# Latent attention: first tiles on free bytes, GpSimd's order written out, a batch's norm moved ahead; first attention: one mask for four diagonal tiles

## The chip, the cores and the metric

The kernel runs on one core of a Trainium2 chip. The metric is the device time of one launch in microseconds (us). Engines are named as in the profile: PE (TensorE matmuls), PEld (its weight loads), DVE (VectorE), ACT (ScalarE), POOL (GpSimd), SP (SyncE, which issues the DMAs). Every engine works through its own queue in order and waits on semaphores for the others.

## The reference

Eight residual layers over x of shape (4, 1024, 128), each applied to a layer norm of x: an attention with a learned position kernel, a mixture of experts (MoE), a linear attention, the same MoE, the latent attention, an expert layer, an attention with relative positions, the same expert layer. The change touches the first and the fifth.

```python
# first attention: 16 heads, causal
scores = jnp.take(causal_kern, jnp.maximum(doff, 0), axis=-1)
scores = scores + qm[..., :, None] + km[..., None, :]
scores = scores + MIX * jnp.einsum('bhic,bhjc->bhij', qc, kc) / math.sqrt(CR)
scores = jnp.where(causal, scores, -1000000000.0)
attn = jax.nn.softmax(scores, axis=-1)
...
# latent attention: 16 heads, causal
c_q = x @ W_DQ
Qc = (c_q @ W_UQ).reshape(B, S, N_HEADS, D_H).transpose(0, 2, 1, 3)
Qr = rope((c_q @ W_QR).reshape(B, S, N_HEADS, D_HR).transpose(0, 2, 1, 3))
c_kv = x @ W_DKV
Kr = jnp.broadcast_to(rope((x @ W_KR)[:, None, :, :]), (B, N_HEADS, S, D_HR))
scores = jnp.clip(jnp.einsum('bhqd,bhkd->bhqk', Q, K), -80.0, 80.0)
scores = jnp.where(causal, scores, -jnp.inf)
weights = jax.nn.softmax(scores / jnp.sqrt(jnp.float32(d_qk)), axis=-1)
attn = jnp.einsum('bhqk,bhkd->bhqd', weights, V)
...
```

## The kernel before

Activations stay in SBUF: 128 tokens on the partitions, eight such tiles for a batch, four batches. In both attentions a "group" is four heads of one batch (16 groups), worked side by side on PE in four blocks of 32 rows. A group has twelve units: the queries come in two halves i of 512 tokens, the keys in tiles jt of 128; half 0 has units jt = 0 to 3, half 1 has jt = 0 to 7. Where the key tile lies in the query half's own range, the unit is cut to the queries that can see it (widths 512, 384, 256, 128) and its first 128 columns are masked causally.

**First attention** (`attn0_heads`). The softmax here takes the row maxima from the scores without the position term. So each slot of the loop holds one "top", which computes scores only to find their maxima, and, ten slots behind (`LEAD`), one `weigh`, which computes the scores again with keys on the partitions, exponentiates them on ACT and multiplies the position factor on POOL (L746); `contract`, three slots later (`LAG`), multiplies by the values on PE (L754). A top is four heads' products (L680) into two score buffers of two PSUM banks each (`pair()`, three of them in all), and one DVE reduce for each buffer (L697). `tops` lists (it, c): query tile it = 0 to 7 against its own half's keys up to and with the diagonal (c = 0, widths 128 to 512; keys lie in reversed order, so the diagonal tile comes first), and for it above 3 against the whole first half (c = 1). For c = 0, four bf16 matmuls (L689) add the causal mask `after` (0 or -1e30) to the 128 diagonal columns. The negated maxima go to `maxima[0]` for it below 4; for the others to `parts`, from which a small reduce (L699) takes the minimum into `maxima[1]`. Five slots into a group `shift(0)`, and at its end `shift(1)`, transposes the maxima on PE (L705) and adds them to the queries (L706).

**Latent attention** (`attn2`). A batch is prepared in pieces: `stats` twice (DVE, L1427 and L1428), `scale` (a square root on ACT, L1436, with its table load; a reciprocal on DVE, L1439; eight multiplications into `xn` on POOL, L1442), and for each half `turn` (transposes, L1458), `latents` (L1475; two copies by ACT into `lq` and `lk`, then two DVE products and one POOL add for the rotary keys, L1467 to L1470), `rotate` (L1483, the same for the rotary queries) and `values` (L1490). Each group projects its heads in four pieces (L1545, L1546). A unit is `weigh` (L1556), a clamp on DVE (two instructions, L1567), an exp on ACT (L1570), for units 0 to 3 and 8 to 11 a causal select on POOL (L1573), and `contract` three units later (L1588). `at(n, piece)` hangs a piece on unit n; a batch's eleven pieces hang on units -22 to -12 before its first. At the end of a batch twelve more pieces divide, turn back and project its output. The pieces take their PSUM from a pool of two banks, of which the running sums of a group hold one.

PE, DVE and ACT follow the order in which the program is written inside `tc.manual_schedule`; POOL is left to the scheduler, and so are, on DVE and ACT, instructions of neighbouring layers, which may be put in between. Tiles get fixed bytes from pools stacked from the left (attentions) or the right (MoE and expert layers); a tile whose bytes were another layer's waits for that layer's last use of them. `vals`, `lq` and `lk` are cleared by POOL at the start (L1389 to L1391), two buffers each. Neighbouring layers share the small tiles of the layer norm (`ln_st`, `ln_mv`, `ln_rs`, two buffers each).

Of the kernel before, what the change touches and what calls it, by code (L numbers as in the profile page):

```python
# [36 lines left out]
P = 128  # L37
# [210 lines left out]
def hybrid_kernel(ctx: ExitStack, tc: tile.TileContext, x, out, blocks, dram, upto=8):  # L248
# [295 lines left out]
    def attn0_heads(W, xn, table, rest):  # L544
# [7 lines left out]
        LEAD, LAG = 10, 3  # L552
        tops = [(it, c) for it in range(TB) for c in range(1 + it // 4)]
        units = [(i, jt) for i in range(2) for jt in range(4 * i + 4)]
        N = len(units)
        with layer_pool("a0h", 2) as pool, layer_pool("a0k", 1) as keep:

            maxima = [keep.tile([P, 4, P], F32, name=f"maxima{n}") for n in range(2)]
            vals = [keep.tile([P, TB, H * 16 + 16], F32, name=f"vals{n}") for n in range(2)]
            for n in range(2):  # L560
                nc.gpsimd.memset(maxima[n], 0.0)
                nc.gpsimd.memset(vals[n], 1.0)
# [83 lines left out]
            class Group:  # L646
# [24 lines left out]

                def top(self, it, c):


                    i = it // 4
                    w = (it % 4 + 1) * P if c == 0 else 512
                    both = [pair().rearrange("p (k w) -> p k w", k=2) for _ in range(2)]
                    for h in range(4):
                        r = slice(32 * h, 32 * h + 32)
                        mm(  # L680
                            both[h // 2][:, h % 2, 0:w],
                            self.q[i][r, (it % 4) * P : (it % 4 + 1) * P],
                            self.k[i - c][r, 512 - w : 512],
                            start=True,
                            stop=c > 0,
                        )
                    if c == 0:
                        for h in range(4):
                            mm(both[h // 2][:, h % 2, 0:P], ident16, after, start=False, stop=True)  # L689
                    if it == 4 and c == 0:  # L690
                        self.parts = pool.tile([P, 4, 4, 2], F32, name="parts")
                    for hp in range(2):
                        if i == 0:
                            o = maxima[0][:, it, 64 * hp + 10 : 64 * hp + 64 : 32]
                        else:
                            o = self.parts[:, it - 4, 2 * hp : 2 * hp + 2, c]
                        nc.vector.tensor_reduce(o, both[hp][:, :, 0:w], AX.X, ALU.max, negate=True)  # L697
                    if it == TB - 1 and c == 1:
                        nc.vector.tensor_reduce(maxima[1][:, :, 10:P:32], self.parts, AX.X, ALU.min)  # L699

# [672 lines left out]
    def attn2(W):  # L1373
# [7 lines left out]
        N = len(units)  # L1381
        with layer_pool("a2", 2) as pool, layer_pool("a2k", 1) as keep:
            vals = [keep.tile([P, TB, H, 32], F32, name=f"vals{n}") for n in range(2)]


            lq = [keep.tile([P, S], F32, name=f"lq{n}") for n in range(2)]
            lk = [keep.tile([64, S], F32, name=f"lk{n}") for n in range(2)]
            for n in range(2):
                nc.gpsimd.memset(vals[n], 1.0)  # L1389
                nc.gpsimd.memset(lq[n], 0.0)  # L1390
                nc.gpsimd.memset(lk[n], 0.0)  # L1391
            extras = {}

            begun, spare = [], []
# [12 lines left out]
            class Batch:  # L1407
# [27 lines left out]
                def scale(self):  # L1435
                    nc.scalar.activation(self.rs, self.rs, AF.Sqrt)  # L1436

                    def later():
                        nc.vector.reciprocal(self.rs, self.rs)  # L1439
                        self.xn = pool.tile([P, TB, D], F32, name="xn", bufs=1)  # L1440
                        for t in range(TB):
                            nc.gpsimd.tensor_scalar(  # L1442
                                self.xn[:, t, :],
                                self.x[:, t, :],
                                self.mv[:, t, 0:1],
                                self.rs[:, t : t + 1],
                                ALU.subtract,
                                ALU.mult,
                            )

                    return later

                def turn(self, i):
                    if i == 0:
                        self.xT = pool.tile([P, S], F32, name="xT", bufs=1)
                    ps = free()
# [155 lines left out]
            for k, group in enumerate(groups[1:], 1):  # L1612
                for j, piece in enumerate(group.pieces):
                    at(N * k - 8 + 2 * j, piece)
                if group.g == 0:
                    for j, piece in enumerate(group.batch.pieces):
                        at(N * k - 22 + j, piece)
            for batch in batches:
                for j, piece in enumerate(batch.ends):
                    at(4 * N * (batch.b + 1) + LAG - 1 + j, piece)  # L1620
            engines = mybir.EngineType
            with tc.manual_schedule(engines={engines.PE, engines.DVE, engines.Activation}):
                first = batches[0]
                for piece in first.pieces[0:3]:
                    run([piece])
                for piece in (first.turn, first.latents, first.rotate):
                    for i in range(2):
                        run([lambda: piece(i)])
# [434 lines left out]
```

## Time and profile before

| | us |
|---|---|
| median of 3 runs | 3723.33 (3722.66 to 3723.78) |
| the profiled execution, whole | 3725.8 |
| its span, first to last instruction | 3724.1 |
| PE busy | 3537.6 (95%) |
| DVE busy | 2079.6 (56%) |
| ACT busy | 1963.5 (53%) |
| POOL busy | 919.6 (25%) |
| mean granted PE clock | 0.974 |
| first attention's heads | about 88 to 853 |
| second MoE layer | about 1402 to 1556 |
| latent attention | about 1556 to 2131 |

The profile is of one execution. A busy PE is not PE at its peak: matmuls are pipelined, their ends are modelled, and a group of them that waits in its middle is shown stretched. The chain of waits follows the work back from the last instruction, at each step to what released it, and gives start, length and what it was ("x8" is eight instructions). In the timeline a bracket holds the idle time of the engine before the instruction and what ended it. Idle time of an engine that nothing waits for costs nothing.

### The profile page before, as it was taken

How to read it: one execution, taken by the hardware profiler on the slowest of the kernel's cores; microseconds unless marked ns; L12 is line 12 of the kernel's file. 1: busy time of each engine (PE TensorE's matmuls, PEld its weight loads, DVE VectorE, ACT ScalarE, POOL GpSimd, SP SyncE). 2: the span in 40 equal slices, each digit the busy share in tenths (PEclk: the TensorE clock that was granted, in tenths of full speed). 3: DMA queues.
4: the chain of work that ended last, by engine and by line, in shares of the span. 5: the costliest groups of instructions: out<-in, count | busy, mean ns of one | idle time of the engine just before them, and what ended most of it. 6: DMA issues, size and time to landing. Idle time of an engine off the chain costs nothing.

```text
span 3724.1 us, 62175 instructions
## 1 busy us (share of the span) xinstructions
PE 3537.6 (95%) x25288; PEld 2046.6 (55%) x25288; DVE 2079.6 (56%) x4986; ACT 1963.5 (53%) x3383; POOL 919.6 (25%) x704
## 2 busy tenths in 40 slices
PE   7999999998999998899999999999999998999999
PEld 3344444436665556633333367666766766766777
DVE  5666666666553445367777721366566566566311
ACT  5455555556422214366666664466566566566543
POOL 4677777772013210222222100001001001000000
PEclk9999999999999999889999999999999999999999
DMA  3111111100520004300000000110111011010000
GB/s 100 43 46 46 46 46 46 46 24 22 142 59 1 1 15 116 91 1 1 1 1 1 14 1 1 58 35 26 33 35 35 24 35 35 24 35 24 4 9 12
DMA packets 95975, 124.31 MB, mean 33 GB/s; under 512 B 3660, under 2 KB 78028, under 8 KB 94536
## 3 DMA queue, kind: packets, MB, share of 16 engines
q1 hardware_dynamic: 95688, 120.33, 10.5%
q8 instruction: 199, 3.26, 0.4%
q14 instruction: 88, 0.72, 0.1%
HBM read 117.59 MB, written 2.73 MB: 32 GB/s over the span
## 4 chain that ended last, share of the span: by engine, by line
PE 83%; DVE 7%; ACT 5%; POOL 2%; issue 1%; DMA 1%; SPq 0%; ACTq 0%; DVEq 0%; POOLq 0%
PE mm L1929 8%; PE s L1879 8%; PE av L1716 6%; PE mm L1706 6%; PE av L1947 6%; PE s L680 5%; PE s L716 5%; PE s L1556 4%; PE av L754 3%; PE av L1097 3%; PE mm L1081 3%; PE av L1588 3%; DVE p L1567 3%; PE av L1545 2%; ACT p L1914 2%; PE av L1306 2%
## 5 line engine op out<-in xcount | busy, mean ns | idle before, releaser
L746 POOL TENSOR_TENSOR p<-p,bias 128x1536 f32<-128x1536 f32 x192 | 504.0, 2629 | 80.3 <-ACT p L728 69.6
L1897 DVE CUSTOM_DVE_ANT_0 p<-s,bias 128x512 f32<-128x512 f32 (+3 forms) x768 | 387.3, 551 | 131.4 <-PE s L1879 124.3
L1567 DVE TENSOR_SCALAR p<-s 128x1024 f32<-128x1024 f32 (+3 forms) x384 | 349.0, 952 | 94.7 <-PE s L1556 93.5
L1914 ACT ACTIVATE p<-p,tops 128x128 f32<-128x128 f32 (+7 forms) x512 | 395.6, 774 | 2.7 <-DVE tops L1897 1.9
L1929 PE MATMUL mm<-ident,p 128*128 128x128 f32 x2304 | 348.8, 284 | 36.1 <-ACT p L1914 32.2
L1934 ACT COPY pt<-mm 128x512 f32<-128x512 f32 (+1 forms) x352 | 185.9, 528 | 368.5 <-PE mm L1929 368.3
L1929 PEld LDWEIGHTS mm<-ident,p 128*128 128x128 f32 x2304 | 249.7, 141 | 173.2 <-issue 64.6
L1570 ACT ACTIVATE p<-p 128x2048 f32<-128x2048 f32 x192 | 281.0, 1483 | 88.8 <-DVE p L1567 85.9
L725 ACT ACTIVATE p<-s 128x1024 f32<-128x1024 f32 x192 | 155.8, 811 | 320.1 <-PE s L716 319.8
L1716 PEld LDWEIGHTS av<-wt,hid 128*128 128x128 f32 x2048 | 263.9, 192 | 107.1 <-issue 107.1
L1962 POOL COPY wide_rec<-rec 128x512 f32<-128x512 f32 x64 | 39.4, 616 | 1120.8 <-DVE rec L1960 1118.3
L697 DVE TENSOR_REDUCE parts<-s 128x2 f32<-128x1024 f32 (+3 forms) x256 | 251.0, 1020 | 105.7 <-PE s L680 59.9
L1879 PE MATMUL s<-keys,q 64*128 64x512 f32 (+3 forms) x1536 | 303.6, 514 | 4.0 <-DVE tops L1897 4.0
L1947 PE MATMUL av<-pt,vals 128*64 128x128 f32 x4608 | 295.2, 278 | 0.0
L1707 ACT ACTIVATE hid<-mm,wt 128x512 f32<-128x512 f32 x256 | 170.8, 691 | 220.7 <-PE mm L1706 220.1
L1947 PEld LDWEIGHTS av<-pt,vals 128*64 128x64 f32 x4608 | 248.8, 137 | 49.6 <-issue 38.5
L1716 PE MATMUL av<-wt,hid 128*128 128x128 f32 x2048 | 264.7, 275 | 0.0
L1706 PE MATMUL mm<-xT,wt 128*128 128x512 f32 x512 | 261.7, 602 | 2.5 <-ACT hid L1707 2.0
L1936 DVE COPY pt<-mm 128x512 f32<-128x512 f32 (+1 forms) x288 | 189.8, 659 | 131.6 <-PE mm L1929 131.3
L1556 PE MATMUL s<-q,k 32*128 32x512 f32 (+3 forms) x1536 | 244.8, 559 | 5.3 <-DVE p L1567 4.0
L680 PE MATMUL s<-k,q 32*128 32x512 f32 (+3 forms) x1536 | 222.8, 536 | 10.6 <-DVE parts L697 5.9
L716 PE MATMUL s<-q,k 32*128 32x512 f32 (+3 forms) x1536 | 224.2, 537 | 0.5 <-ACT p L728 0.3
(398 smaller groups left out, 5386.8 us busy)
## 6 DMA issues: line engine op xcount, KB each, us to landing
root<-roots SPq DMA_DIRECT2D x128, 256.0 KB, 6.1
bias<-rel_dram SPq DMA_DIRECT2D x32, 1024.0 KB, 5.5
bias<-pos_dram SPq DMA_DIRECT2D x16, 1536.0 KB, 7.1
bias<-pos_dram SPq DMA_DIRECT2D x16, 512.0 KB, 8.0
wt<-w_ffn SPq DMA_DIRECT2D x2, 2132.0 KB, 8.1
wt<-w_ffn SPq DMA_DIRECT2D x2, 1192.0 KB, 5.2
wt<-w_attn SPq DMA_DIRECT2D x1, 2336.0 KB
x_sb<-x SPq DMA_DIRECT2D x4, 512.0 KB, 6.9
```

Of the source, the lines that this page charges most:

```text
L680: mm(both[h // 2][:, h % 2, 0:w], self.q[i][r, (it % 4) * P : (it % 4 + 1) * P], self.k[i - c][r, 512 - w : 512], start=True, stop=c > 0,)
L716: mm(both[h // 2][:, h % 2, 0:w], self.k[jt // 4][r, (3 - jt % 4) * P : (4 - jt % 4) * P], self.q[i][r, w0:512], start=True, stop=True,)
L746: nc.gpsimd.tensor_tensor(d, d, self.bias[:, 0:3, u : u + w], ALU.mult)
L1556: mm(both[h // 2][:, h % 2, 0:w], self.k[r, jt * P : (jt + 1) * P], self.q[r, 512 * i + w0 : 512 * (i + 1)], start=True, stop=True,)
L1567: nc.vector.tensor_scalar(pt[:, 2 * hp : 2 * hp + 2, 0:w], both[hp][:, :, 0:w], 80.0, -80.0, ALU.min, ALU.max)
L1706: mm(ps, W("w1")[:, c * P : (c + 1) * P], self.batch.xT[:, self.i * 512 : (self.i + 1) * 512], start=True, stop=True)
L1716: mm(o, self.hid[:, c, t * P : (t + 1) * P], W("w2")[:, c * P : (c + 1) * P], start=(c == 0), stop=(c == C - 1))
L1879: mm(s[:, kk, 0:e], self.q[r, it * P : (it + 1) * P], keys[self.n][r, S - n + c : S - n + c + e], start=True, stop=True,)
L1897: nc.vector.tensor_tensor_reduce(out=self.p[it][:, kk, c : c + e], in0=s[:, kk, 0:e], in1=self.bias[:, kk, c : c + e], scale=-1.0, scalar= ...
L1914: nc.scalar.activation(p, p, AF.Exp, bias=self.top[it][:, kk : kk + 1], scale=-1.0, accum_out=self.sums[:, it, kk : kk + 1])
L1929: nc.tensor.transpose(ps[:, m, kk, :], self.p[it][:, kk, (m0 + m) * P : (m0 + m + 1) * P], ident)
L1947: mm(self.acc[64 * kk : 64 * kk + 64, (it % 4) * P : (it % 4 + 1) * P], vals[self.n][:, it - m0 - m, :], pt[:, m, kk, :], start=(m0 + m == 0),
```

## The change

Four edits:

1. First attention: the twelve tops of a group are listed anew. The four diagonal tiles of a half become one top (`"diagonal"`): sixteen products of 128 keys into the two score buffers, one tile for each 128 columns, then four mask matmuls of 512 columns (`after` repeated four times), then two reduces that give a maximum for each tile. The keys before the diagonal tile in the own half (`"own"`, widths 128, 256, 384) and the first half's keys for the second (`"before"`, 512) are tops with no mask. All maxima go to `parts[i]`, now kept for the whole layer and set to the largest value once, and a small reduce follows for both halves.
2. Latent attention, bytes: the long-lived tiles' pool is opened first and so lies leftmost, with `xn` and `xT` (now single, kept tiles) and `lq`, `lk` ahead of `vals`.
3. Latent attention, POOL: its engine joins the written order. Clearing `vals[0]` stands behind the first batch's norm, clearing `vals[1]` hangs on unit 4.
4. Latent attention, pieces: a batch's eleven pieces hang on units -36, -35, -34 (statistics and norm), -29 (turn), -27 (latents), -25 (rotate), -23 (values) for the first half, and -22, -19, -13, -11 for the second.

```diff
-        tops = [(it, c) for it in range(TB) for c in range(1 + it // 4)]
+        tops = [("diagonal", 0)] + [("own", it) for it in (1, 2, 3)] + [("diagonal", 1), ("before", 4)]
+        tops += [(kind, it) for it in (5, 6, 7) for kind in ("own", "before")]
...
+            parts = [keep.tile([P, 4, 4, 2 + n], F32, name=f"parts{n}") for n in range(2)]
             for n in range(2):
+                nc.gpsimd.memset(parts[n], -LOWEST)
...
+                def top(self, kind, n):
                     both = [pair().rearrange("p (k w) -> p k w", k=2) for _ in range(2)]
...
+                    if kind == "diagonal":
+                        for t in range(4):
+                            for h in range(4):
+                                r = slice(32 * h, 32 * h + 32)
+                                mm(
+                                    both[h // 2][:, h % 2, t * P : (t + 1) * P],
+                                    self.q[i][r, t * P : (t + 1) * P],
+                                    self.k[i][r, (3 - t) * P : (4 - t) * P],
+                                    start=(t == 0),
+                                    stop=False,
+                                )
                         for h in range(4):
-                            mm(both[h // 2][:, h % 2, 0:P], ident16, after, start=False, stop=True)
+                            mm(both[h // 2][:, h % 2, :], ident16, wide(after, 4), start=False, stop=True)
+                    else:
+                        w, keys = (t * P, self.k[i]) if kind == "own" else (512, self.k[0])
...
                     for hp in range(2):
+                        if kind == "diagonal":
+                            o = parts[i][:, :, 2 * hp : 2 * hp + 2, 0].rearrange("p t h -> p h t")
+                            x = both[hp].rearrange("p k (t w) -> p k t w", t=4)
                         else:
+                            o = parts[i][:, t, 2 * hp : 2 * hp + 2, 1 if kind == "own" else 2]
+                            x = both[hp][:, :, 0:w]
+                        nc.vector.tensor_reduce(o, x, AX.X, ALU.max, negate=True)
+                    if kind != "diagonal" and n == (3 if i == 0 else 7) and (i == 0 or kind == "before"):
+                        nc.vector.tensor_reduce(maxima[i][:, :, 10:P:32], parts[i], AX.X, ALU.min)
...
-        with layer_pool("a2", 2) as pool, layer_pool("a2k", 1) as keep:
-            vals = [keep.tile([P, TB, H, 32], F32, name=f"vals{n}") for n in range(2)]
+        with layer_pool("a2k", 1) as keep, layer_pool("a2", 2) as pool:
+            normed = keep.tile([P, TB, D], F32, name="xn")
+            turned = keep.tile([P, S], F32, name="xT")
             lq = [keep.tile([P, S], F32, name=f"lq{n}") for n in range(2)]
             lk = [keep.tile([64, S], F32, name=f"lk{n}") for n in range(2)]
+            vals = [keep.tile([P, TB, H, 32], F32, name=f"vals{n}") for n in range(2)]
             for n in range(2):
-                nc.gpsimd.memset(vals[n], 1.0)
                 nc.gpsimd.memset(lq[n], 0.0)
                 nc.gpsimd.memset(lk[n], 0.0)
+            def clear(n):
+                nc.gpsimd.memset(vals[n], 1.0)
...
                 if group.g == 0:
-                    for j, piece in enumerate(group.batch.pieces):
-                        at(N * k - 22 + j, piece)
+                    for j, piece in zip((36, 35, 34, 29, 27, 25, 23, 22, 19, 13, 11), group.batch.pieces):
+                        at(N * k - j, piece)
...
-            with tc.manual_schedule(engines={engines.PE, engines.DVE, engines.Activation}):
+            with tc.manual_schedule(engines={engines.PE, engines.DVE, engines.Activation, engines.Pool}):
                 first = batches[0]
                 for piece in first.pieces[0:3]:
                     run([piece])
+                clear(0)
+                at(4, lambda: clear(1))
```

More of the change, by code (lines that the diff above doesn't have):

```diff
@@ L670, in keys @@
                     nc.scalar.activation(self.k[i], ps, AF.Identity, bias=W("bk")[:, self.g : self.g + 1])
-                def top(self, it, c):
-                    i = it // 4
-                    w = (it % 4 + 1) * P if c == 0 else 512
+                def top(self, kind, n):
                     both = [pair().rearrange("p (k w) -> p k w", k=2) for _ in range(2)]
[L678 to L687, printed above, removed]
-                        for h in range(4):
-                            mm(both[h // 2][:, h % 2, 0:P], ident16, after, start=False, stop=True)
-                    if it == 4 and c == 0:
-                        self.parts = pool.tile([P, 4, 4, 2], F32, name="parts")
+                    i = n if kind == "diagonal" else n // 4
+                    t = n % 4
+                    if kind == "diagonal":
[9 more added lines that the diff above has]
+                                )
+                        for h in range(4):
+                            mm(both[h // 2][:, h % 2, :], ident16, wide(after, 4), start=False, stop=True)
+                    else:
+                        w, keys = (t * P, self.k[i]) if kind == "own" else (512, self.k[0])
+                        for h in range(4):
+                            r = slice(32 * h, 32 * h + 32)
+                            mm(
+                                both[h // 2][:, h % 2, 0:w],
+                                self.q[i][r, t * P : (t + 1) * P],
+                                keys[r, 512 - w : 512],
+                                start=True,
+                                stop=True,
+                            )
@@ L692, in top @@
                     for hp in range(2):
-                        if i == 0:
-                            o = maxima[0][:, it, 64 * hp + 10 : 64 * hp + 64 : 32]
-                        else:
[L696 to L699, printed above, removed]
+                        if kind == "diagonal":
+                            o = parts[i][:, :, 2 * hp : 2 * hp + 2, 0].rearrange("p t h -> p h t")
+                            x = both[hp].rearrange("p k (t w) -> p k t w", t=4)
+                        else:
+                            o = parts[i][:, t, 2 * hp : 2 * hp + 2, 1 if kind == "own" else 2]
+                            x = both[hp][:, :, 0:w]
@@ L1439, in later @@
                         nc.vector.reciprocal(self.rs, self.rs)
-                        self.xn = pool.tile([P, TB, D], F32, name="xn", bufs=1)
+                        self.xn = normed
                         for t in range(TB):
@@ L1453, in turn @@
                 def turn(self, i):
-                    if i == 0:
-                        self.xT = pool.tile([P, S], F32, name="xT", bufs=1)
+                    self.xT = turned
                     ps = free()
```

## The prediction

> **What bounds the kernel now.** I read the busy times first (PE 95% of the span), then the busy times by stage, since one share over eight layers says nothing about two of them.
>
> ```profile
> 88.00:853.00 765.00, 742.73 (x5655) 299.50 (x5652) 511.08 (x746) 394.25 (x706) 578.45 (x325) 0.99 0.13 44
> 1556.00:2131.00 575.00, 527.60 (x3557) 182.44 (x3556) 407.33 (x592) 364.24 (x343) 131.74 (x180) 0.93 0.01 5
> ```
>
> After the window: its length, then busy us of PE, PE's loads, DVE, ACT, POOL, then the granted clock. The first attention (first line) is PE's: 742.7 of 765 us at a clock of 0.99. The latent attention (second) has 47 us without PE and a clock of 0.93: time is lost in it. Where, the same view tells for single stretches; the stretches of the heads are cut at the first clamp of a group of four heads.
>
> ```profile
> 1556.33:1588.35 32.02, 21.01 (x44) 8.62 (x44) 6.87 (x10) 5.83 (x10) 17.46 (x16) 0.57 0.19 68
> 1621.28:1648.68 27.40, 27.31 (x204) 8.50 (x200) 21.83 (x25) 20.27 (x18) 5.00 (x9) 1.00 0.00 1
> 1648.68:1693.51 44.83, 38.92 (x232) 12.54 (x224) 30.39 (x50) 27.45 (x28) 15.32 (x20) 0.89 0.00 1
> 1785.11:1829.82 44.71, 38.98 (x232) 12.52 (x224) 30.30 (x50) 27.45 (x28) 15.32 (x20) 0.89 0.00 1
> 1921.42:1971.24 49.82, 42.18 (x232) 13.35 (x224) 34.14 (x86) 32.89 (x34) 15.34 (x20) 0.83 0.00 1
> ```
>
> From the last matmul of the MoE layer to the first scores of the latent attention: 32.0 us at a clock of 0.57. A plain group: 27.4. The three groups that prepare the next batch: 44.8, 44.7, 49.8, so 17.4, 17.3 and 22.4 more. The chain of waits shows what the first of these hangs on:
>
> ```profile
> 1556.43 0.95 POOL lk L1391
> 1557.38 3.45 POOL vals L1389
> 1560.83 0.89 POOL lq L1390
> 1561.73 0.89 POOL lk L1391
> 1562.62 6.25 POOL xn L1442 x8
> ...
> 1576.95 1.27 POOL lq L1470
> 1578.22 0.04 issue
> 1578.27 2.07 PE s L1545 x2
> 1580.34 2.00 PE av L1545 x2
> ```
>
> POOL's clears stand ahead of the norm; one (lk) waited for the MoE layer's last matmul. The chain also has "POOL xn" at 1661.66, 1797.97 and 1934.95: the later batches' norms, placed one unit ahead of the transposes that need them.
>
> **Start of the latent attention: -16 us.** The timeline has batch 0's 1/std (L1439) done at 1474.6; only POOL's queue and the bytes hold the norm. Afterwards the clears of lq and lk (4 x 0.95) and the norm (6.25) fit between 1475 and 1490, hidden by 66 us of MoE matmuls, in which POOL does nothing else. What is late next: the transposes wait for PSUM that the last residual add frees (L1106, 1556.35 + 0.69 = 1557.04). Then two transposes (0.59 each), copy (0.59), two latent products (1.06 each), copies to lq and lk (4 x 0.58), four DVE pairs (1.37 each) of which the third feeds the add that releases the projections: 1557.1 + 0.59 + 0.59 + 0.1 + 1.06 + 1.16 = 1560.6, + 3 x 1.4 = 1564.8, + 1.27 = 1566.1, where the chain above has 1578.22: 12.1 earlier. The projections and values behind it took 10.1 us (1578.27 to 1588.35) at a clock of 0.50; at full clock 5.0, and the first group, at half clock up to 1601, gains up to 4. With all of it -21, with none -12; PE still has a hole of 3 us before the projections, so I take the middle, -16. The clear of vals0 (3.5), now behind the norm, runs while PE transposes; vals1's goes to unit 4, after which four units give POOL nothing: hidden; without that cover 3.5 each.
> The Trainium skill ("TensorE: Matmul & The Clock Gate", part 1 on the HAM clock gate) has the full clock back after about 3.4 us of busy PE. Here the clock stood at 0.50 from 1564 to 1600 although PE was busy without a break from 1578 to 1590; the trace disagrees. By the page a drop of the clock at that hole would cost 1.7 us and no more, and the item would be -19.
>
> **Three later batches: -13 us.** What can go, from the group at 1648.68: PE idle around sqrt, table loads and norm (1661 to 1665, 1.61 us busy of 4: 2.4, and 1.2 of sparse transposes); the half clock behind it (0.50 over 5 us, 0.68 over 5 us: 2.5 + 1.6); waits of pieces in neighbouring units for one PSUM bank (idle before PE at 1678.5, 1680.3, 1687.0, 1690.9: 0.52 + 0.68 + 0.68 + 1.35 = 3.2). Sum 10.9; with the chain's 0.7 of ACT ahead of the sqrt 11.6. What comes back: units 0 to 3 of a group are where PE waits for DVE's clamps (in the chain 2.26, 1.79, 0.70 in a row), and the statistics (8 x 0.46 = 3.7, and 0.17) now stand in units 0 and 1; the chain before paid 1.55 of them, so +2.3. The second rotation's DVE pair (1.4) now ends a group just ahead of that place: +1.4. And POOL's written order puts unit 3's causal select behind the norm. From the clamp of unit 0: clamps and statistics to 8.0, sqrt between two table loads of 1.28 to 10.2, exp of unit 2 to 11.3, its select to 11.9, norm to 18.2, select of unit 3 to 18.8; PE wants unit 3 in unit 6 at about 16.2: 2.7 late (queued behind: PE's contraction, then the copy of the sums on ACT). So -11.6 + 6.4 = -5.2 for batches 1 and 2. The third carries more of the next layer:
>
> ```profile
> 1941.22 0.31 DVE L345 BATCH_NORM_AGGREGATE ln_mv<-ln_st 128x2 f32<-128x6 f32 x3 [5.45 <-POOL xn L1442]
> ```
>
> This is the following expert layer's layernorm, put into DVE's order while POOL still read the buffer it needs. The buffers are the same afterwards, so I keep most of it: -3. Bounds: all waits gone, 3 x 11.6 + 5 = -40; nothing gained, 0.
>
> **First attention: +2 us.** Prices from the chain in one group:
>
> ```profile
> 302.57 0.43 PE s L680 x8
> 303.01 0.33 PE s L689 x4
> ...
> 305.03 0.77 PE s L680 x8
> ...
> 308.15 0.88 PE s L680 x8
> ...
> 312.48 1.07 PE s L680 x8
> 313.55 0.33 PE s L689 x4
> 313.88 0.57 PE av L754 x8
> 314.45 1.77 PE s L716 x8
> ```
>
> Eight L680 instructions are four heads' products of 128, 256, 384, 512 keys; L689 is the mask. Half a group, before: 0.43 + 0.77 + 0.88 + 1.07 + 4 x 0.33 = 4.47. After: sixteen diagonal products, 4 x 0.43 = 1.72; masks of 512 columns; own keys 0.43 + 0.77 + 0.88 = 2.08. No row has such a mask: at the time per instruction of the narrow one 0.33, at its time per column 1.32; I take the middle, 0.85, since L689 also carries a weight load each (98 ns). Sum 4.65, +0.18 a half, 32 halves: +6 (-11 to +21). The reduces on DVE keep their widths (2 x 1.22, 0.42, 0.69, 0.95); 16 more small ones (0.19 each) hide on an engine busy 32.2 of 46.4 us. Then the waits: 1.77 above is 1.07 of matmul and 0.7 of waiting for a score buffer that DVE reduces; such stretches are some 4.6 us of 46.4. A diagonal tile of 2.6 us on PE gives DVE and ACT time to free buffers in two of twelve slots, and the slots with no mask start the reduce earlier, but two reduces start later: I take -0.2 a group, -4, with 1 us either way (16). Together +2, from -20 to +25.
>
> **Sum.** -16 - 13 + 2 = -27. The profiled execution took 3725.8 (span 3724.1 and 1.7 around it), 2.5 above the median of the runs, 3723.3. 3725.8 - 27 = 3698.8, on the median's scale 3696.
>
> **Rivals.**
> (a) *The norm on POOL becomes the wait.* If unit 3's select comes so late that PE's clock drops again, each batch pays the 4.1 us of half clock once more: 3 x 4.1 = 12, total -15, 3708. For: POOL's order is now strict and the 6.25 us come whole. Against: 2.7 us of idle against 4 at the drops seen.
> (b) *Slower: diagonal products don't overlap.* Four heads' products run side by side today; cut into sixteen, each with its own weights, they might run one by one. The row for that: 32 instructions of 128 f32 columns in 3.57 us (L1840), so 3.57 for a tile in place of 1.72; 32 tiles, +59; total +32, 3755. Against: 128-key products now take 0.43 for eight. It decides from 27 us / 1024 instructions = 26 ns more in each, 80 instead of 54.
> The Trainium skill speaks for (b): by the same page ("LDWEIGHTS") a load lasts columns / 1.2, 107 ns for 128, whatever the rows, 3.4 us for 32 loads in a row; the row of 0.43 for eight loads and products disagrees unless they overlap.
> (c) *The first tiles still wait*: if norm or transposed tile share bytes with the MoE layer, the norm starts right after the MoE layer, near 1557.5 instead of 1562.6, and PE is as cold as now: -5 - 13 + 2 = -16, 3707.
> (d) *More goes*: every wait named for the batches falls (-25, between -13 and -40) and the first attention's waits go with them (-18, near its lower end): -16 - 25 - 18 = -59, 3664.
>
> **How the numbers follow.** Forecast 0.54, (a) 0.17, (b) 0.10, (c) 0.08, (d) 0.11. The forecast's own range is 3678 to 3714. 3664 to 3722 takes in (a), (c) and (d) and leaves out (b) and some spread on both sides, 2 in 10. 0.2% (7.4 us) is about what a measurement can tell from no change. Faster than 3715.9: most of the forecast, (a), (c), all of (d), 0.78; within, 0.11; slower, (b) and the tail of the first attention's bounds, 0.11.
>
> **What would show it.** Right: "xn" on POOL near 1475 and off the chain; first scores about 16 us sooner after the MoE layer's last matmul; batch groups of 38 to 40 us; L689 down from 512 matmuls to 128, of 512 columns each; group period of the first attention at 46 to 47. Wrong: a PE wait on L1573's select beside "xn"; a clock of 0.5 after it; diagonal tiles over 3 us; DVE's 5.45 gone or grown. The prediction fails if the first attention's group moves by over 1 us, which outweighs everything in the later stage.

## The result, and the profile after

| | before | after |
|---|---|---|
| median, us | 3722.99 (3721.82 to 3723.78, 4 runs) | 3700.35 (3697.01 to 3704.87, 4 runs) |
| ratio | | 0.994, 95% interval 0.9923 to 0.9957 |
| profiled execution, span | 3724.1 | 3695.3 |
| first attention, first scores to last contraction | 767.6 | 762.5 |
| three layers in between (untouched) | 693.8 | 691.7 |
| MoE's last run of products to first scores of the latent attention | 41.1 | 29.3 |
| its first group, to the copy of its sums | 38.6 | 39.6 |
| its other fifteen groups | 492.6 | 486.0 |
| the three last layers (untouched) | 1604.6 | 1601.6 |

22.6 us were gained where 27 were forecast. The touched stages of the two profiles give 5.1 + 11.7 - 1.0 + 6.6 = 22.4. The untouched ones (and 1.2 us ahead of the first attention) differ by another 6.3, which is what one profile differs from the next, as the experiments will show. That the touched stages sum to nearly the gain of the medians is luck: stages with the same code differ by several us between profiles.

The busy times by stage of the kernel after, cut here at the second copy of a group's sums, L1621 (window, its length, busy us of PE, PE's loads, DVE, ACT, POOL, granted clock):

```profile
86.00:846.50 760.50, 732.77 (x6028) 306.79 (x6026) 509.07 (x764) 398.72 (x706) 578.37 (x325) 0.99 0.14 45
...
1547.95:1568.19 20.24, 15.27 (x41) 6.57 (x40) 6.87 (x10) 5.83 (x10) 5.03 (x4) 0.70 0.29 108
1607.76:1645.44 37.68, 34.33 (x224) 10.82 (x224) 26.10 (x34) 25.36 (x27) 13.71 (x18) 0.87 0.00 1
1645.44:1677.21 31.77, 29.38 (x220) 9.67 (x220) 24.92 (x30) 22.70 (x24) 7.52 (x10) 1.00 0.00 1
1742.18:1778.95 36.77, 33.44 (x224) 10.82 (x224) 26.84 (x34) 25.07 (x26) 13.72 (x18) 0.91 0.00 1
1778.95:1810.72 31.77, 29.38 (x220) 9.68 (x220) 24.92 (x30) 22.71 (x24) 7.52 (x10) 1.00 0.00 1
1876.39:1921.83 45.44, 37.77 (x224) 11.67 (x224) 29.75 (x61) 30.77 (x32) 13.71 (x18) 0.81 0.00 1
1921.83:1953.60 31.77, 29.38 (x220) 9.68 (x220) 24.92 (x30) 22.71 (x24) 7.52 (x10) 1.00 0.00 1
```

The stretch ahead of the first scores fell from 32.0 to 20.2 us. The groups come in pairs now. Groups 1, 5 and 9, which carry the statistics, the norm, and the first transposes, products and rotation, last 37.7, 36.8 and 45.4 us where before, at the same cut, they were plain and lasted 27.4, 27.9 and 27.9 (groups 1 and 9 of the kernel before):

```profile
1626.92:1654.32 27.40, 27.31 (x204) 8.50 (x200) 21.86 (x25) 20.27 (x19) 5.00 (x8) 1.00 0.01 1
1899.17:1927.06 27.89, 27.80 (x208) 8.70 (x210) 22.31 (x27) 20.27 (x20) 5.00 (x8) 1.00 0.01 1
```

Groups 2, 6 and 10 fell to 31.8 from 44.8, 44.7 and 49.8. The work was not removed, it moved one group ahead, and it costs nearly as much there (10.3, 8.9 and 17.5 us, against 13.0, 12.9 and 18.0 gained).

The chain of waits at the start:

```profile
1547.99 0.70 DVE x_sb L1124
...
1548.83 0.64 PE s L1481 x4
...
1555.38 0.68 DVE lq L1490
...
1556.10 0.70 DVE other L1491
...
1556.87 1.27 POOL lq L1493
...
1558.18 2.07 PE s L1568 x2
...
1568.26 2.06 PE s L1579 x8
```

No clear and no norm is left in it: the norm ran from 1466.5 to 1472.8 under the MoE layer. What stands there now is DVE's rotations, of which the first projection needs the third. The ten us from 1558.18 to 1568.26 are as long as before.

The timeline in group 1, where statistics and norm now stand:

```profile
1604.44 1.80 DVE L1590 TENSOR_SCALAR p<-s 128x768 f32<-128x768 f32 x2
...
1605.44 0.70 PE L1579 MATMUL s<-q,k 32*128 32x256 f32 x4 [1.59 <-DVE p L1590]
...
1607.88 0.17 DVE L1455 TENSOR_SCALAR ln_rs<-ln_mv 128x8 f32<-128x8 f32 x1
...
1608.34 1.28 ACT L1460 ACT_TABLE_LOAD   x1
...
1608.71 0.80 PE L1579 MATMUL s<-q,k 32*128 32x128 f32 x4 [1.79 <-DVE p L1590]
...
1609.86 1.28 ACT L1593 ACT_TABLE_LOAD   x1
...
1612.90 6.23 POOL L1466 TENSOR_SCALAR xn<-x_sb,ln_mv,ln_rs 128x128 f32<-128x128 f32 x8
...
1619.78 0.43 PE L1611 MATMUL av<-p,vals 128*32 128x128 f32 x8 [0.63 <-POOL p L1596]
```

PE waits 1.59 and 1.79 us for clamps that stand behind statistics, and the granted clock is 0.50 from 1607.15 to 1613.97: it falls behind the first of these waits, ahead of the two table loads. At the norm's end PE waits 0.63 us for the select of unit 3, and the clock is at 0.50 once more from 1620.80 to 1624.21. In groups 5 and 9 the clamps' waits are 2.38 and 2.88 us, and PE does not wait for a select.

The chain in a group of the first attention:

```profile
299.33 1.10 PE s L688 x32
300.43 0.97 PE s L696 x4
...
303.58 0.43 PE s L701 x8
...
306.03 0.67 PE s L701 x8
...
309.63 1.02 PE s L701 x8
...
313.25 1.39 PE s L688 x32
```

The sixteen diagonal products of the first half take 1.10 us, 34 ns for each of 32 instructions, and the four masks of 512 columns 0.97: 2.07 for the tile. Those of the second half, at 313.25, take 1.39. So it is in every group: in the trace all 16 tiles of the first half take 1.10, and those of the second 1.34 to 2.01 (2.63 once, at half clock), since the two heads that go to the second score buffer start late there. The mean is 1.40.

### The profile page after: what moved, and what is told of

It reads as the page before. It is cut to its first block, busy times and chain, and to the rows that moved or that the text cites. A ratio compares the mean times of both kernels' runs of the same rounds, so it can differ in the third digit from the quotient of the medians.

```text
span 3695.3 us, 62973 instructions
## 1 busy us (share of the span) xinstructions
PE 3499.6 (95%) x25672; PEld 2039.6 (55%) x25672; DVE 2077.0 (56%) x5002; ACT 1966.8 (53%) x3383; POOL 919.2 (25%) x706
## 4 chain that ended last, share of the span: by engine, by line
PE 83%; DVE 6%; ACT 6%; issue 2%; POOL 2%; DMA 1%; SPq 0%; ACTq 0%; DVEq 0%; POOLq 0%
PE mm L1955 8%; PE s L1905 8%; PE av L1742 6%; PE mm L1732 6%; PE av L1973 6%; PE s L734 5%; PE s L701 4%; PE s L1579 4%; PE av L772 3%; PE av L1115 3%; PE mm L1099 3%; PE av L1611 3%; ACT p L1940 2%; PE av L1568 2%; PE av L1324 2%
## 5 line engine op out<-in xcount | busy, mean ns | idle before, releaser
L715 DVE TENSOR_REDUCE parts<-s 128x2 f32<-128x1024 f32 (+4 forms) x384 | 349.9, 952 | 151.2 <-PE s L701 89.0
L1973 PEld LDWEIGHTS av<-pt,vals 128*64 128x64 f32 x4608 | 248.0, 137 | 49.6 <-issue 38.6
L701 PE MATMUL s<-k,q 32*128 32x512 f32 (+3 forms) x1280 | 179.1, 510 | 10.3 <-DVE parts L715 7.0
```

What stands on the lines that cost most here:

```text
L715: nc.vector.tensor_reduce(o, x, AX.X, ALU.max, negate=True)
L1973: mm(self.acc[64 * kk : 64 * kk + 64, (it % 4) * P : (it % 4 + 1) * P], vals[self.n][:, it - m0 - m, :], pt[:, m, kk, :], start=(m0 + m == 0),
```

## The experiments

Each was timed against the kernel before on its own chip; the ratios are to that kernel. The stages below come from one profile of each, cut as in the table above. They are read stage by stage, because stages with the same code differ from profile to profile: the three layers in between from 688.4 to 699.3, the first attention with the changed code from 762.5 to 766.0.

| kernel | ratio, 95% interval | first attention | in between | to first scores | group 0 | groups 1 to 15 |
|---|---|---|---|---|---|---|
| before | 1 | 767.6 | 693.8 | 41.1 | 38.6 | 492.6 |
| after | 0.9940 (0.9923 to 0.9957) | 762.5 | 691.7 | 29.3 | 39.6 | 486.0 |
| attn0_only | 0.9996 (0.9987 to 1.0005) | 765.9 | 694.4 | 40.8 | 39.2 | 495.5 |
| diag_heads | 1.0078 (1.0064 to 1.0092) | 810.4 | 692.6 | 29.3 | 41.0 | 484.3 |
| old_bytes | 0.9981 (0.9970 to 0.9992) | 762.5 | 699.3 | 37.6 | 40.1 | 490.4 |
| pool_auto | 0.9946 (0.9929 to 0.9962) | 766.0 | 688.4 | 29.3 | 41.0 | 487.8 |
| warm | 0.9934 (0.9922 to 0.9947) | 762.7 | 692.3 | 26.7 | 38.3 | 489.6 |
| start_order | 0.9950 (0.9938 to 0.9963) | 766.0 | 692.5 | 28.0 | 39.7 | 492.7 |
| old_slots | 0.9969 (0.9957 to 0.9980) | 762.7 | 692.4 | 29.3 | 39.3 | 495.6 |
| norm_moved | 0.9976 (0.9966 to 0.9986) | 762.9 | 689.4 | 29.3 | 40.0 | 493.2 |
| spread | 0.9916 (0.9902 to 0.9930) | 763.1 | 692.4 | 29.3 | 41.1 | 474.1 |
| own_stats | 0.9925 (0.9913 to 0.9938) | 762.8 | 698.9 | 29.3 | 41.1 | 477.5 |
| best | 0.9873 (0.9854 to 0.9891) | 766.0 | 694.2 | 24.6 | 37.5 | 468.7 |

### The first attention by itself

The kernel before with edit 1 of the change and none of the others.

> The kernel before with the first attention's edit alone. Theory from the two traces: the sixteen diagonal products overlap across the four heads even better than eight did, so the first attention gains 5 us and the rest stays: 3718 of 3723. The prediction's term: +2, 3725. Rival (products one by one): +59 or more, 3782. If the 23 us come from the latent attention alone, the stage of the first attention lasts as long as before (group period 46.4); by the theory 46.1.

3718.66 us against 3719.11: -1.5 us by the ratio, from -4.8 to +1.9. The profile's first attention is 1.7 us shorter than before. So the edit brings little, and the 22 us come from the latent attention. The 5 us that the two first profiles differ by are the upper end of what this code shows: eleven profiles of it have 762.5 to 766.0.

### The diagonal products in another order

```diff
-                        for t in range(4):
-                            for h in range(4):
+                        for h in range(4):
+                            for t in range(4):
```

> The changed kernel with the sixteen diagonal products of a tile in order of heads (four tiles of one head in a row, all on the same 32 rows) in place of tiles (four heads in a row, on four sets of 32 rows). Theory: the 1.10 us for 32 instructions (34 ns each) come from products of different heads running side by side; in a row on the same rows they go one by one, 32 x 107 to 112 ns as in rows of single 128-column products = 3.5 us a tile, 32 tiles, +77 us: 3777. Rival: the order doesn't matter, 3700.

The chain of this kernel in one group:

```profile
317.36 2.75 PE s L688 x32
320.11 0.97 PE s L696 x4
```

2.75 us for the same 32 instructions, 86 ns each; the mask is the same. In the traces the 32 tiles together take 88.7 us in place of 44.7 (each from the end of the work before it to its own), 44 more; the first attention grew by 48, and the kernel is slower than before. The rival in the prediction that came out slower needed products one by one, more than 80 ns an instruction: this is it, and what keeps the change from it is that products of different heads, on different rows, follow each other. My 3.5 us a tile were too many.

### Which edit brings the norm forward

`old_bytes` takes the norm's output and the transposed tile from the layer's running tiles again:

```diff
-        with layer_pool("a2k", 1) as keep, layer_pool("a2", 2) as pool:
-            normed = keep.tile([P, TB, D], F32, name="xn")
-            turned = keep.tile([P, S], F32, name="xT")
+        with layer_pool("a2", 2) as pool, layer_pool("a2k", 1) as keep:
...
-                        self.xn = normed
+                        self.xn = pool.tile([P, TB, D], F32, name="xn", bufs=1)
```

> The changed kernel with the norm's output and the transposed tile back on the bytes of before (taken from the buffers of the layer's running tiles, behind the MoE layer's), GpSimd's order and the slots as changed. Theory: it is the free bytes that let the first norm run at 1466, 66 us before the MoE layer ends; on the old bytes it waits for the MoE layer's last matmuls, and the 6.25 us, with what waits behind them, stand on the path again: first scores 9 to 12 us later after the MoE layer's last matmul (38 to 41 us in place of 29.3), 3709 to 3712. Rival: the written order of GpSimd (clears behind the norm) gave it: 29 to 33 us, under 3704.

`pool_auto` leaves GpSimd out of the written order:

```diff
-            with tc.manual_schedule(engines={engines.PE, engines.DVE, engines.Activation, engines.Pool}):
+            with tc.manual_schedule(engines={engines.PE, engines.DVE, engines.Activation}):
```

> The changed kernel without GpSimd in the list of engines whose order is written out. Theory: the written order decides nothing that the path sees at the start (the norm has 66 us of cover) and costs at most the select of unit 3 behind the norm (PE idle 0.63 us there and the clock's second fall): -3 to +1, 3697 to 3701. Rival: left to itself GpSimd runs the norm late again, as before: batches and start fall back, 3706 or more.

The chain of `old_bytes`:

```profile
1556.01 0.44 POOL lk L1407
...
1558.74 6.22 POOL xn L1462 x8
1565.00 0.48 PE s L1478
...
1574.36 2.08 PE s L1565 x2
```

The norm stands in the path again, with the last clears of `lq` and `lk` ahead of it, and the first scores come after 37.6 us in place of 29.3. 8.3 of the 11.7 us are thus the bytes; the other 3.5 fit one clear of `vals` (3.45 in the chain before), which the program now puts behind the norm. Without the written order the start is the same to 0.01 us (29.34), the norm at 1467.5: writing out GpSimd's order gives nothing there, and the time can't be told from that of the kernel after. Nor does it make the wait for a select: left to the scheduler, PE waits 1.28 us for one in group 1, against 0.63. `old_bytes` is timed 15 us behind the kernel after, and so above the 3709 to 3712 expected. The start shows 8.3 of it; the 4.4 of groups 1 to 15 lie within that stage's spread, the 7.6 in between are in untouched layers, and so the rest stays open.

### What halves the clock at the start

`warm` puts matmuls that nobody reads into the hole ahead of the first projection:

```diff
+                def warm():
+                    ps = free()
+                    for _ in range(7):
+                        mm(ps, W("wx"), turned[:, 0:512], start=True, stop=True)
...
-                    run([lambda: first.values(i)] + groups[0].pieces[2 * i : 2 * i + 2])
+                    run([lambda: first.values(i)] + [warm] * (i == 0) + groups[0].pieces[2 * i : 2 * i + 2])
```

> The changed kernel with seven more matmuls of 512 columns, read by nobody, in the 3.8 us in which TensorE waits for the rotated latents at the start of the latent attention. Theory: this hole is what halves the clock; with it filled the projections take 5 us in place of 10.1 and the first group is not cold for 12 us: first scores 5 us sooner, the first group's end 8 to 11 sooner, 3691 against 3700. Rival: the clock falls for another reason (the wait before the transposes, 0.9 us, or the sparse matmuls behind them), and stays at 0.50: 0 to +1.

`start_order` fills nothing, and lets the first batch's queries be rotated ahead of its keys:

```diff
-                for piece in (first.turn, first.latents, first.rotate):
-                    for i in range(2):
-                        run([lambda: piece(i)])
+                for i in range(2):
+                    run([lambda: first.turn(i)])
+                keys = [first.latents(i) for i in range(2)]
+                for i in range(2):
+                    first.rotate(i)()
+                    keys[i]()
```

> The changed kernel with the first batch's rotations of queries ahead of those of keys on DVE and GpSimd at the start of the latent attention, so that the first projection waits for the first of four pairs and not for the third. Theory: two pairs of 1.4 us sooner, 2.8 us; and if the hole of 3.8 us in TensorE is what halves the clock, a hole of 1.1 us leaves it at 1.00 and 5 to 8 us more go: 3688 to 3692. Rival: the clock falls all the same: 2.8 us, 3697.

Stretches of 4 us, first of the kernel after (the hole is 1554.3 to 1558.2), then of `warm`; the clock is the third number from the end. Behind them the filling in `warm`, and what is left of the hole in `start_order`, in PE's timeline:

```profile
1552.00:1556.00 4.00, 2.33 (x13) 1.26 (x12) 3.35 (x5) 2.27 (x4) 1.82 (x2) 0.99 0.68 290
1556.00:1560.00 4.00, 1.82 (x2) 0.50 (x2) 2.14 (x4) 0.00 (x0) 3.20 (x3) 0.50 0.00 0
1560.00:1564.00 4.00, 4.00 (x11) 2.27 (x10) 0.00 (x0) 1.17 (x2) 0.00 (x0) 0.50 0.00 0
...
1572.00:1576.00 4.00, 3.64 (x16) 1.64 (x14) 2.92 (x4) 2.73 (x2) 0.64 (x1) 0.50 0.00 2
1576.00:1580.00 4.00, 3.65 (x20) 1.22 (x20) 1.65 (x4) 2.35 (x3) 2.58 (x4) 0.52 0.01 4
```

```profile
1558.00:1562.00 4.00, 4.00 (x11) 1.75 (x10) 1.92 (x3) 0.00 (x0) 2.96 (x3) 1.00 0.00 0
1562.00:1566.00 4.00, 4.00 (x15) 1.74 (x13) 0.00 (x0) 1.75 (x3) 0.00 (x0) 1.00 0.00 0
...
1570.00:1574.00 4.00, 3.42 (x18) 1.59 (x18) 3.54 (x5) 3.07 (x2) 0.63 (x1) 0.66 0.02 6
1574.00:1578.00 4.00, 4.00 (x20) 1.05 (x20) 1.13 (x3) 1.90 (x3) 3.11 (x4) 0.50 0.00 0
```

```profile
1556.02 6.28 PE L1658 MATMUL s<-xT,wt 128*128 128x512 f32 x14
```

```profile
1560.06 2.08 PE L1568 MATMUL s<-lq,wt 128*128 128x512 f32 x2 [1.79 <-POOL lq L1493]
```

With the hole filled the clock stays at 1.00 and the projections take 5.2 us (1562.13 to 1567.33) in place of 10.1: without the matmuls in the hole the clock falls, with them it doesn't. Of this only 2.6 us reach the first scores, since seven matmuls took 6.3 us in a hole of 3.8, and 1.3 more the end of group 0, since the clock falls again where PE waits for the first clamps. By the ratios `warm` gains 2 us on the kernel after, within their intervals, where 9 were expected. In `start_order` the hole is 1.8 us, and the clock falls to 0.50 all the same, at 1558.88, only 0.6 us into it, after 3.4 us in which PE had been without work for 0.63. So the length of the hole does not decide alone; that the matmuls just ahead of it, on 32 rows, count for less than the filling's on 128 would fit, and is not shown. The first projection comes 2.1 us sooner than in the kernel after, the values behind it wait 0.7 for a copy on ACT, and 1.3 are left at the first scores. The time is no better than the kernel after's (0.9950 against 0.9940), outside what both readings expected. Its groups 1 to 15 have the slots of the kernel after and 492.7 us, against 486.0: so wide is the spread of that stage.

### The slots

> The changed kernel with the batch's eleven pieces back at the units of before (22 to 12 ahead, one each). Theory: the earlier slots brought only some 5 us over three batches, since what the batch's own group gained (10 to 17 us) was lost in the group where statistics and norm now stand; so 3705 against 3700, and groups 1, 5 and 9 back at 27.4 to 28.5, groups 2, 6 and 10 at 42 to 45. Rival: the slots are worth the 13 us that were predicted and something else costs 8: 3713. Other rival: the slots cost, and the new bytes give the gain: under 3697.

`old_slots` has `zip((22, 21, 20, 19, 18, 17, 16, 15, 14, 13, 12), group.batch.pieces)`. Groups 1, 5 and 9 are back at 27.4, 27.9 and 27.9 us, groups 2, 6 and 10 at 44.8, 44.7 and 51.9. The three profiles with the old slots (before, `attn0_only`, `old_slots`) have 492.6, 495.5 and 495.6 us for groups 1 to 15, mean 494.6; the six with the new ones and no other edit behind the start (after, `warm`, `start_order`, `diag_heads`, `old_bytes`, `pool_auto`) 484.3 to 492.7, mean 488.5. That is 6 us for the slots; the medians, 0.9969 and 0.9940 of 3719, say 11, with intervals that touch. More than nothing, less than the 13 predicted.

`norm_moved` takes the statistics out of units 0 and 1 and puts the norm into unit 4: `zip((39, 37, 32, 27, 25, 23, 21, 19, 17, 13, 11), group.batch.pieces)`.

> The changed kernel with the statistics in units 9 and 11 of the group ahead, where DVE idles 1.2 to 1.3 us a unit, and 1/std with the norm in unit 4, behind which four units ask no select of GpSimd; transposes and the rest follow two units later than in the changed kernel. Theory: the statistics in units 0 and 1 (PE idle 1.59 + 1.79), the clock's fall behind them and the select behind the norm are what groups 1, 5 and 9 lose (10.2, 8.6, 17.7 us); so 5 to 8 us a batch, 3676 to 3685 against 3700. Rival: DVE and ACT carry that work wherever it stands, and the loss only moves to another group: 3697 to 3703.

The theory, as far as this placing goes, fell: 3711.55 us, and groups 1 to 15 at 493.2. Group 1 did fall, to 34.1, but group 2 rose to 37.5:

```profile
1608.08:1642.18 34.10, 31.30 (x204) 9.07 (x196) 23.38 (x28) 24.79 (x25) 12.50 (x17) 0.90 0.00 1
1642.18:1679.67 37.49, 35.78 (x236) 12.63 (x236) 25.90 (x32) 23.07 (x23) 8.83 (x11) 0.86 0.00 0
```

The clock is at 0.50 from 1616.53 to 1623.36, behind the square root: DVE's reciprocal waits 1.52 us for it and its table load, the next clamps stand behind the reciprocal, and PE idles 0.84 us for them. It is there again from 1643.84 to 1654.08, behind two rotations in units 11 and 1: their DVE products stand in the chain ahead of the clamps, and PE idles 1.23 and 1.31 us. So it is not the statistics alone: in these places too, what DVE or ACT is given where PE waits for clamps costs a wait and then the clock.

`spread` therefore looks for each engine's idle places, from the timeline of a plain group: ACT waits 3 to 4 us ahead of the exp of unit 0, GpSimd has no select in units 4 to 7, DVE idles 1.3 us ahead of the clamp of unit 4.

```diff
-                    self.pieces = [lambda t=t: self.stats(t) for t in (0, 4)] + [self.scale]
+                    self.pieces = [lambda t=t: self.stats(t) for t in (0, 2, 4, 6)] + [self.scale, self.norm]
...
-                        for t in range(t0, t0 + 4):
+                        for t in range(t0, t0 + 2):
...
+                    return lambda: nc.vector.reciprocal(self.rs, self.rs)
+
+                def norm(self):
...
-                    for j, piece in zip((36, 35, 34, 29, 27, 25, 23, 22, 19, 13, 11), group.batch.pieces):
+                    for j, piece in zip((45, 43, 41, 39, 36, 33, 27, 21, 19, 15, 24, 17, 13, 11), group.batch.pieces):
```

> The changed kernel with the batch's preparation laid where each engine idles: statistics in four pieces of two tiles in group 0 of the batch before (units 3, 5, 7, 9), sqrt with its two table loads in unit 0 of group 1, where ScalarE waits 3 to 4 us for a clamp, the norm in unit 3 behind the last select, transposes at unit 9 and at unit 0 of group 2, the rotations' DVE pairs in units 3, 5, 7 and 11. Theory: what groups 1, 5 and 9 lose is DVE work and table loads in places where TensorE waits for DVE's clamps, and the half clock behind them; so groups 1 and 5 fall from 37.7 and 36.8 to about 30, group 2 rises by 2 at most: 4 to 6 us a batch, 3682 to 3688 against 3700. Rival: DVE and ACT carry the work wherever it stands: 3697 to 3705, as the move of statistics and norm alone came out 7 us behind the changed kernel.

Groups 1 and 2 of this kernel:

```profile
1611.90:1641.08 29.18, 29.09 (x212) 9.21 (x208) 21.19 (x23) 21.23 (x21) 11.18 (x16) 0.94 0.00 1
1641.08:1677.40 36.32, 33.19 (x232) 11.03 (x224) 27.44 (x34) 23.89 (x25) 10.06 (x12) 0.95 0.00 0
```

Groups 1, 5 and 9 fell to 29.2, 27.6 and 39.2, groups 2, 6 and 10 rose to 36.3, 34.7 and 34.7: more than the 2 us expected, since projections waited 0.91, 1.17 and 0.71 us for the PSUM bank that a rotation in the unit before still held. In all 12 us less in groups 1 to 15 than the kernel after, below every profile with its slots, and 3691.85 us, short of the 3682 to 3688 expected. Statistics, table loads, norm and rotations all moved at once here, so what each is worth is not shown.

### The third batch

```diff
-                            self.st = small.tile([P, TB, 6], F32, name="ln_st")
-                            self.mv = small.tile([P, TB, 2], F32, name="ln_mv")
+                            self.st = small.tile([P, TB, 6], F32, name="a2_ln_st")
+                            self.mv = small.tile([P, TB, 2], F32, name="a2_ln_mv")
...
-                            self.rs = small.tile([P, TB], F32, name="ln_rs")
+                            self.rs = small.tile([P, TB], F32, name="a2_ln_rs")
```

> The changed kernel with tiles of their own names for the latent attention's mean, variance and 1/std, which it shared with the layernorms of the other layers. Theory: group 9 lasts 45.4 us where groups 1 and 5 last 37.7 and 36.8, because the next expert layer's layernorm, put into DVE's order there, waits 6.64 us on GpSimd for the shared buffer; with buffers of its own group 9 falls to about 38 and the kernel by 6 to 8 us, 3693 against 3700. Rival: the layernorm waits for something else or lands in another bad place: 0, 3700.

DVE's timeline in group 9 of the kernel after shows what this takes away:

```profile
1888.38 0.58 DVE L345 BATCH_NORM_AGGREGATE ln_mv<-ln_st 128x2 f32<-128x6 f32 x7 [6.64 <-POOL xn L1466]
```

The next layer's layernorm holds DVE for 6.64 us until GpSimd's norm lets go of the shared buffer, and the clamps behind it wait too. With separate buffers the same instruction follows its neighbours without a wait:

```profile
1886.91 0.17 DVE L345 BATCH_NORM_AGGREGATE ln_mv<-ln_st 128x2 f32<-128x6 f32 x1
```

Group 9 lasts 36.6 us in place of 45.4, as groups 1 and 5 do: the cause is shown. By the ratios the kernel (3695.31 us, 0.9925) gains 5.6 on the kernel after, with intervals that overlap.

### All three together

Slots of `spread`, buffers of `own_stats`, and four matmuls in the hole.

> The spread slots, statistics in buffers of their own, and four matmuls that nobody reads in the hole at the start, together. Theory: the three act in different places, so their gains in the latent attention add up: from its 554.9 us in the changed kernel 10.4 for the slots, 8 for group 9's layernorm (39.2 there to about 30), 4 to 6 for the hole (the seven matmuls took 6.3 us in a hole of 3.8 and so delayed the projections by 2.3; four take 3.5): 530 to 534; the kernel 3676 to 3680. Rival: the layernorm only moves to another place of DVE once the slots are spread, 3684 to 3688.

3676.24 us, 47 less than before and 25 less than after by the ratios. From the MoE layer's last products to the last copy of sums it takes 530.9 us (24.6, 37.5 and 468.7 in the table; after: 554.9). Windows of this kernel: the start, groups 5, 6, 9 and 10.

```profile
1554.28:1569.82 15.54, 14.20 (x50) 6.38 (x49) 6.86 (x10) 5.84 (x10) 5.04 (x4) 1.00 0.38 140
...
1739.45:1768.70 29.25, 28.39 (x212) 8.95 (x208) 22.58 (x31) 23.92 (x25) 11.19 (x16) 1.00 0.01 1
1768.70:1805.03 36.33, 33.19 (x232) 11.02 (x224) 27.45 (x34) 23.92 (x26) 10.07 (x12) 0.95 0.00 0
1871.96:1901.21 29.25, 28.39 (x212) 8.96 (x208) 22.58 (x31) 23.92 (x25) 11.18 (x16) 1.00 0.00 1
1901.21:1935.94 34.73, 31.58 (x228) 10.86 (x224) 27.37 (x33) 23.92 (x25) 10.07 (x12) 1.00 0.00 1
```

The clock is 1.00 from the MoE layer to the first scores, and group 9 is a group like group 5.

## Why the prediction was right, and where it was not

The sign, the likeliest case and the order of the sum were right. Each of its three terms was off: the two of the latent attention promised more than came, by 4 to 5 and 2 to 7 us, the first attention's less, by 3.5. That the sum lies nearer than its terms is luck.

- **Start, -16.** It measured -11.7 to the first scores, and group 0 gave nothing (39.6 us against 38.6). The mechanism was right: norm and clears left the chain, and the last addition to `lq` ended at 1558.14, 0.4 us from where 1566.1 comes to lie when the 8.4 us are taken off by which this execution was ahead. The size was wrong by the choice of the middle between the cold end and the warm one. I counted a hole of 3 us ahead of the projections and gave the clock half a chance in it; it fell, as in every profile in which the hole was not filled.
- **Start, which edit.** The prediction had the bytes free the norm and the clears stand behind it; the runs split this into 8.3 and 3.5. The written order of GpSimd, which rival (a) was built on, made no difference that the time shows.
- **Three later batches, -13.** -6 to -11. The gains came about as predicted where the work left (13 to 18 us in groups 2, 6 and 10, part of it work that moved along); the failed step is the price where it went. I took +2.3 for the statistics, +1.4 for a rotation, +2.7 for the select behind the norm, and the half clock as gone. The select costs 0.63 in one group of three; the statistics cost 1.59 + 1.79 of waiting and, behind the first of these waits, the half clock once more, which I had counted among the gains: group 1 runs at 0.87 over 37.7 us, which I estimate at 4.9 us. I had set 2.7 us of idle against 4 at the drops seen, and that was misread: the trace of the kernel before has the clock fall at 1662.95, 1799.49 and 1936.02 after 3.4 us in which PE was without work for 1.45, 1.67 and 1.10. Rival (a) had this fall of the clock in it, but from the norm on GpSimd: right effect, and, but for the second fall in group 1, the wrong engine.
- **Third batch, -3.** The layernorm was named, and its wait was kept; it grew from 5.45 to 6.64 us. It could be had back by three names of tiles.
- **First attention, +2.** -1.5 by the run that has it alone, from -4.8 to +1.9. The diagonal products were mis-sized: I took four times the 0.43 us of eight instructions, 1.72, and undisturbed they take 1.10, or 1.40 in the mean with the second half's waits for a buffer. The 0.43 holds a fixed part that a longer row pays once: in the trace the four sets of rows start 7 ns behind one another and each set again 112 ns later, so 24 more instructions add 6 x 0.112 = 0.67 us. The mask, 0.85 by choice between 0.33 and 1.32, took 0.97. All tops together take 262.7 us on PE before and 254.3 after (256.8 in `attn0_only`), each from the end of the work before it: 8.4 and 5.9 less, of which the first attention's length shows 5.1 and 1.7. Where the rest went was not traced.
- **Signs.** Three of those named for being wrong came: a wait on the select beside the norm, the clock at 0.50 behind it (both in group 1), and the layernorm's wait grown. The batch groups of 38 to 40 us became pairs of groups, with 31.8 in the second.
- **Rival (b)** needed 80 ns an instruction; 34 were measured (44 with the waits inside), and 86 with the two loops exchanged. **(c)** fell with the norm at 1466. **(d)** did not come, though `best` shows that more of those waits can be removed.

## What to carry to other kernels

Work that is moved off a critical path is paid again where it lands: price it in the new place by what the path waits for there, engine by engine, and look for the units in which that very engine is idle. Where the clock falls behind waits of 1 to 2 us, as in these traces, a wait costs more than its length, and work that nobody reads can be cheaper than a hole. Small matmuls on part of the rows should be written so that neighbours use different rows.

## What the hardware showed unexpectedly

**Small products overlap by rows.** 32 instructions of 32 rows x 128 columns take 1.10 us when four sets of rows take turns, 2.75 when the same rows follow each other. In both traces instructions on the same rows start 107 to 112 ns apart once the row runs, and those on other rows 4 to 7 ns behind one another; the mean of 86 in the slow order comes from the ends of the heads, where two sets of rows run side by side. The Trainium skill ("TensorE: Matmul & The Clock Gate", part 3, on the mechanism) says that a weight load overlaps with matmuls in flight only where their row groups differ. The spacing in the two runs fits that; since the ends of matmuls are modelled, they do not show what the same rows wait for. The columns / 1.2 that the same page of the Trainium skill has for a load ("LDWEIGHTS"), by estimate 107 ns for 128 columns, which the prediction weighed as a price for each, are close to the spacing on the same rows, and are no price for each where the rows differ (34).

**The clock falls early and comes back late.** In all thirteen traces the clock is 1.00 or 0.50, and a stretch of one clock lasts a whole multiple of 3.41 us (but for the last, cut off by the end). In the latent attention it fell at the end of such a 3.41 us with as little as 0.63 us without work on PE (`start_order`, ahead of 1558.88; after, ahead of 1620.80), and stayed up through others with 1.35 (before, ahead of 1970.15): idle time alone does not decide. It came back only behind 3.41 us with at most 0.30 without work, but not behind each: in the kernel after it stayed at 0.50 from 1555.95 to 1579.84, seven times 3.41 us, though PE was busy throughout from 1558.18 to 1569.60. The same page of the Trainium skill (part 1, the two states) has the clock fall after an idle window of about 3.4 us and rise after about 3.4 us of sustained work. The step of 3.41 us shows in these traces; but less idle time sufficed for the fall, and that much work did not always bring the rise. What ends the slow stretch is not settled by these runs.
